# A graph layer with experts: mixing's rows accumulated into x in DRAM, and one expert group of tiles run densely instead of two

## The chip, the cores and the metric

The kernel runs on one core of one Trainium2 chip. The metric is device time in microseconds (us) of one execution; shorter is better. Before the change it is 2823.4 us, the median of three runs (2821.6 to 2824.84).

## The reference

3125 nodes with 512 features, 53125 directed edges (25000 random pairs in both directions, and one loop at each node). Cut to what matters:

```
xn  = layernorm(x)
x   = x + gnn(xn, edges) + mix(xn)
out = x + experts(layernorm(x))

gnn:      two layers; in each, attention over the edges with 8 heads of 64 (softmax over a
          node's incoming edges), Wo, batch norm over the nodes, ff 512->128->512, batch norm;
          after both a layer norm
mix:      linear attention over all nodes; q and k are softmaxed, out = (q ctx)/den + q, then Wp
experts:  p = softmax(z Wg + bg); each node keeps its two best of 8 experts
          out = sum over these e of p_e * (gelu(z W1_e + b1_e) W2_e + b2_e)
```

## The kernel before, in words

Nodes are sorted by their number of edges and cut into 25 tiles of 128 (the last has 53). `FGROUPS` are seven groups of `GT` = 4 tiles, g0 to g6; g6 is the one tile of 53 rows. Two groups, g5 and g6 (`STAY`), remain in SBUF between the steps of a layer, the others go through a DRAM tile `xmid`.

**Edges of the second layer (attention, L508).** A tile's edges are taken in chunks of `G` = 2 slots. For each chunk POOL starts one or two indirect gathers of K and V rows (L591, `lane<-kvd,idx`), DVE multiplies K by q (L596) and sums (L597); after the softmax, ACT (L632) or DVE (L635) weighs V, and TensorE adds up (L647, L652). There are four lanes with six places each; the gather of a chunk goes over the K half of an earlier one, so it waits for its L597, and over the V of one earlier still. POOL takes its instructions in order, as all engines do, so a gather also waits for whatever stands ahead of it there. Beside the edges, in small steps of a generator, runs the mixing: `mixed` (L809 to L858), nine steps for each of 25 tiles. How many steps go between two chunks is a count written in the loop (L891 to L921). Its last step copies the rows y from PSUM on ACT (L856) and stores them to a DRAM tile `base` through SP's queue (L857). Another DRAM tile, `xb`, holds x plus the bias of the mixing and that of the last layer norm, by node; it is written at the start of the kernel (L369).

**After the edges**, batch norms and the ff run over the groups (L926 to L968; L943 is ACT's half of the norm, with scale and bias by feature), in the order g5, g6, g0, ... (`FORDER`). Then `last` (L990):

- `gates(group)` is a generator (L1025). For each tile it turns features to rows (`ps`, TensorE L1044, ACT copy L1046) and takes statistics (`row_stats`, DVE L476, L477). It gathers rows of `base` and of `xb` (two indirect gathers on POOL, L1056) and adds them on POOL (L1059), and forms y on DVE (L1061, L1063), with statistics again. Then z, the normalized rows, on DVE (L1072); z goes to DRAM (`zld`) if the tile is listed; four transposes of z (`tr`, L462) with a copy that alternates between ACT (L454) and DVE (L456); the gate product `pg` (L1080) and its bias (L1082). Then softmax, ranks and the choice of two for the group (L1089 to L1106), and the second biases, comb times b2, added to `yall` (L1108 to L1119). All copies of `pg`, of `pc` and of some others share one PSUM bank.
- Two groups run **densely**, g5 and g4 (`ALL_EXPERTS`): all their nodes go through all eight experts (`all_experts`, L1127: `ph` L1134, gelu L1137, `py` L1141, weighted sum on DVE L1143) and are stored by an indirect DMA (`put`, L1123).
- The other 17 tiles (`LISTED`, `NL`) are **listed**: DVE forms lists of nodes by expert (`lists`, L1149), with a loop of 2 x 17 rounds of one DVE operation (L1217) and one product on `pw` (L1219), which gives `which` (L1222). 40 parts (`PARTS`) of 128 rows then go through one expert each (`one_expert`, L1233): POOL gather of z rows (L1236), transposes and copy (L462, L464), `ph` (L1243), the first bias as a product of a row of ones and b1 in fp32 (L1245), gelu (L1250), transpose `pt` (L1252) and copy (L1253), `py` (L1255), copy (L1257), store to `yld` by SP (L1258).
- In the end, for each listed tile, two gathers from `yld` (L1291), two weighted sums on DVE (L1294) and a put.

The driver (L1260 to L1297) sets the order: gates of g5; gates of the other groups, and after each third `yield` one dense expert of g5; lists; gates of g4 and three of its dense experts; the 40 parts; the five experts that are left, with g4's puts; the final loop over listed tiles. The order within one engine's queue is mostly that of the program, with a scheduler that moves some instructions ahead where their inputs are ready.

Of the kernel before, what the change touches and what calls it, by code (L numbers as in the profile page):

```python
# [1 line left out]

# [55 lines left out]

ALL_EXPERTS = [FGROUPS[STAY[0]], FGROUPS[4]]
LISTED = [t for g in FGROUPS if g not in ALL_EXPERTS for t in TILES[g[0]:g[0] + g[1]]]  # L60
# [32 lines left out]
def gps_layer(ctx: ExitStack, tc: tile.TileContext, x, src, dst, cols, rows,  # L93
# [15 lines left out]
    recd = tc.dram_tile([FT * P, 4], I32, name="recd")  # L109
    base = tc.dram_tile([N, D], F32, name="base")  # L110
    zd = tc.dram_tile([N, D], F32, name="zd")
# [285 lines left out]
    with tc.If(flag < 1) as fits:  # L397
        listed_layers(tc, cols=cols, rec=rec, idx=idx, mask=mask, kvd=kvd, zd=zd, ztd=ztd, xb=xb,
                      base=base, wqo=wqo, layer_weights=layer_weights, **args)
    with fits.Else():  # L400
# [17 lines left out]
def listed_layers(ctx: ExitStack, tc: tile.TileContext, rows,  # L418
                  gnn_wq, gnn_wk, gnn_wv, gnn_wo, gnn_w1, gnn_w2,
                  mix_wq, mix_wk, mix_wv, mix_wp, wg, bg, w1, w2, b2, out,  # L420
                  ident, epst, colt, cols, rec, idx, mask, kvd, zd, ztd, xb, base,
                  wqo, layer_weights):
# [85 lines left out]
    def attention(l, stats, wq, wo, mixw):  # L508
        with tc.tile_pool(name="att", bufs=1, reuse_waits="tile") as ap, \
# [299 lines left out]
            def mixed(t):  # L809
# [46 lines left out]
                nc.scalar.copy(y[:n], ps[:n])  # L856
                nc.sync.dma_start(base[t * P:t * P + n, :], y[:n])  # L857
                yield  # L858
# [113 lines left out]
    def load_experts(fp):  # L972
        w1t = fp.tile([128, NX, NP, FX], F32, name="w1t")
        w2t = fp.tile([FX, NX, D], F32, name="w2t")
        for e in range(NX):
            nc.sync.dma_start(w1t[:, e], w1[e].rearrange("(c p) f -> p c f", p=128))
            nc.sync.dma_start(w2t[:, e, :], w2[e])
        b2t = fp.tile([NX, D], F32, name="b2t")
        nc.sync.dma_start(b2t, b2)
        wgt = fp.tile([128, NP, NX], F32, name="wgt")  # L980
        nc.sync.dma_start(wgt, wg.rearrange("(c p) e -> p c e", p=128))
        bgt = fp.tile([P, NX], F32, name="bgt")
        nc.sync.dma_start(bgt, rows_by_partition(bg, 0, P))
        gt = fp.tile([P, D], F32, name="gt")
        nc.sync.dma_start(gt, rows_by_partition(rows, ROW_G, P))
        b1t = fp.tile([1, NX, FX], F32, name="b1t")
        return w1t, w2t, b2t, wgt, bgt, gt, b1t


    def last(xT, w1t, w2t, b2t, wgt, bgt, gt, b1t):  # L990
        with tc.tile_pool(name="fin", bufs=1, reuse_waits="tile") as fp, \
# [19 lines left out]
                           allow_small_or_imprecise_dtypes=True)  # L1011

            b1p = pp.tile([NX, FX], F32, name="b1p", tag="pg", bufs=1)
            nc.tensor.transpose(b1p, colt[:, XB1:XB1 + NX], ident)
            b1s = fp.tile([NX, FX], F32, name="b1s")
            nc.scalar.copy(b1s, b1p)
            b1d = tc.dram_tile([NX, FX], F32, name="b1d")
            nc.sync.dma_start(b1d, b1s)
            nc.sync.dma_start(b1t, b1d.rearrange("(o e) f -> o e f", o=1))
            steps = fp.tile([P, NL], F32, name="steps")  # L1020
# [4 lines left out]
            def gates(t0, k):  # L1025
# [15 lines left out]
                for i, (t, n) in enumerate(tiles):  # L1041
# [5 lines left out]
                    row_stats(fp, yall[:n, t, :], mv[:n, i, :])  # L1047
                yield
                inv = fp.tile([P, GT], F32, name="sd_y", bufs=2)
                nc.scalar.activation(inv, mv[:, :, 1], AF.Sqrt, bias=epst)  # L1050
                nc.vector.reciprocal(inv, inv)
                for i, (t, n) in enumerate(tiles):
                    bt = fp.tile([P, D], F32, name="bt", bufs=4)
                    bx = fp.tile([P, D], F32, name="bx", bufs=3)
                    for o, held_in in ((bt, base), (bx, xb)):
                        nc.gpsimd.indirect_dma_start(  # L1056
                            out=o[:n], out_offset=None, in_=held_in[:, :],
                            in_offset=bass.IndirectOffsetOnAxis(ap=node(t), axis=0))
                    nc.gpsimd.tensor_add(bt[:n], bt[:n], bx[:n])  # L1059
                    y = yall[:n, t, :]  # L1060
# [4 lines left out]
                    row_stats(fp, y, mv2[:n, i, :])  # L1065
                yield
                sd = fp.tile([P, GT], F32, name="sd_z", bufs=2)
                nc.scalar.activation(sd, mv2[:, :, 1], AF.Sqrt, bias=epst)
                nc.vector.reciprocal(sd, sd)
                for i, (t, n) in enumerate(tiles):  # L1070
                    z = fp.tile([P, D], F32, name="z", bufs=3)
                    nc.vector.tensor_scalar(z[:n], yall[:n, t, :], mv2[:n, i, 0:1], sd[:n, i:i + 1],  # L1072
                                            op0=OP.subtract, op1=OP.mult)
# [8 lines left out]
                    nc.vector.tensor_add(prob[:n, i, :], pg[:n], bgt[:n])  # L1082
                yield

                prob, rank = prob[:, :k, :], rank[:, :k, :]
                m = fp.tile([P, GT], F32, name="pm", bufs=2)
                m = m[:, :k]
                wide = [P, k, NX]
                nc.vector.tensor_reduce(m, prob, AX.X, OP.max)  # L1089
# [7 lines left out]
                for e in range(NX):  # L1097
                    more = fp.tile([P, GT, NX], F32, name="more", bufs=2)
                    pe = prob[:, :, e:e + 1]
                    nc.vector.tensor_tensor(more[:, :k, :e + 1], pe.to_broadcast([P, k, e + 1]),  # L1100
                                            prob[:, :, :e + 1], OP.is_gt)
                    if e + 1 < NX:
                        nc.vector.tensor_tensor(more[:, :k, e + 1:], pe.to_broadcast([P, k, NX - 1 - e]),
                                                prob[:, :, e + 1:], OP.is_ge)
                    nc.vector.tensor_add(rank, rank, more[:, :k, :])
                nc.vector.scalar_tensor_tensor(prob, rank, 1.5, prob, op0=OP.is_lt, op1=OP.mult)  # L1106
                yield
                combT = fp.tile([NX, GT * P], F32, name="combT")  # L1108
# [4 lines left out]
                nc.vector.tensor_copy(combT[:, :w], pc[:, :w])  # L1113

                for i, (t, n) in enumerate(tiles):
# [3 lines left out]
                    nc.vector.tensor_add(yall[:n, t, :], yall[:n, t, :], pb[:n])  # L1119
                yield prob  # L1120

# [27 lines left out]
            def lists():  # L1149
# [8 lines left out]
                    for a, b in ((0, 2), (2, 3), (3, 5), (5, 7))]  # L1158
                both = both[0]

                end = LISTED[-1][1]
# [47 lines left out]
                room = xT.tiles[2].rearrange("p c r -> p (c r)")  # L1209
                hot = room[:, 4 * P:4 * P + 2 * NL * PARTS].rearrange("p (j q) -> p j q", q=PARTS)  # L1210
                nc.vector.tensor_tensor(hot, digf[:, 1, :, None].to_broadcast([P, 2 * NL, PARTS]),
# [3 lines left out]
                for j in range(2 * NL):  # L1215
                    low = room[:, j % 4 * P:(j % 4 + 1) * P]
# [16 lines left out]
            def one_expert(part, e, which):  # L1233
# [25 lines left out]

            def weights(g):  # L1260
                for prob in gates(*g):
                    pass
                return prob

            work = all_experts(*ALL_EXPERTS[0], weights(ALL_EXPERTS[0]))
            ready = 0
            for g in FGROUPS:
                if g not in ALL_EXPERTS:
                    for _ in gates(*g):
                        ready += 1  # L1270
                        if ready % 3 == 0:
                            next(work, None)
            for _ in work:
                pass
# [11 lines left out]
            for _ in work:  # L1286
                pass
            for u, (t, n) in enumerate(LISTED):
                for i in range(2):
                    y1 = xT.tiles[3][:, (2 * u + i) % 4, :]  # L1290
                    nc.gpsimd.indirect_dma_start(  # L1291
# [624 lines left out]
```

## Time and profile before

| | |
|---|---|
| median of three runs | 2823.4 us |
| profiled execution, its own time | 2825.41 us |
| its span | 2823.7 us |
| TensorE busy | 2319.8 us, 82% |
| VectorE (DVE) busy | 2029.8 us, 72% |
| ScalarE (ACT) busy | 1394.9 us, 49% |
| GpSimd (POOL) busy | 1482.8 us, 53% |
| TensorE clock, mean | 0.888 of full |

The profile is one execution, slightly longer than the median. Its span runs from the first to the last recorded instruction. Stages, in us from the span's start: edges of the second layer 1336 to 2240, norms and ff to 2327, gates to 2516, ranks and lists to 2544, the loop on `pw` to 2570, up to the first part to 2607, the parts to 2729, the tail to the end. In a row of a timeline stand start, duration, engine, line, operation, output and inputs, and in brackets how long the engine had been idle and what ended that. PE is TensorE's product, PEld its weight load. fp32 products are recorded as two instructions each. A row of waits reads: engine, tile and line that waited, what for, total us, times, longest.

### The profile page before, as it was taken

The page shows a single profiled execution, that of the slowest core. Times are in us where ns is not written, and L with a number is a line of the kernel's source. Part 1 is how long each engine was busy: PE and PEld are TensorE (multiplying, and loading weights), DVE is VectorE, ACT ScalarE, POOL GpSimd, SP SyncE. Part 2 cuts the span into 40 slices and gives each one's busy share as a digit, 9 for nine tenths or more (in the row PEclk, how much of TensorE's full clock was granted, in tenths as well). Part 3 has the DMA queues.
Part 4 walks back from the last instruction along what each step waited for, and adds up shares of the span by engine and source line. Part 5 has one row for each costly group of instructions (what it writes and reads, how often), then busy time and mean ns, then how long its engine had stood idle before and what let it go on. Part 6 is the DMA issues. An engine that isn't in the chain of part 4 may idle for free. (4 is left out here: it accounts for less than half of the span.)

```text
span 2823.7 us, 31795 instructions
## 1 busy us (share of the span) xinstructions
PE 2319.8 (82%) x9096; PEld 1306.3 (46%) x9096; DVE 2029.8 (72%) x3245; ACT 1394.9 (49%) x5341; POOL 1482.8 (53%) x1231
## 2 busy tenths in 40 slices
PE   6987989889889867999697788888977576869992
PEld 3432435545445544344345455555544334436750
DVE  7810989999999986401879888999987577774333
ACT  1111578788777753201467677787766333211210
POOL 3261788888777860011657666666765205420336
PEclk9998999999999988999799898989989787766996
DMA  8434989999999874422978888989977513210554
GB/s 286 169 119 142 336 324 332 330 329 334 341 327 341 319 238 149 163 80 80 321 257 310 294 319 285 333 302 327 329 269 252 158 32 103 88 56 29 170 152 148
DMA packets 229275, 654.54 MB, mean 232 GB/s; under 512 B 50968, under 2 KB 56477, under 8 KB 224991
## 3 DMA queue, kind: packets, MB, share of 16 engines
q0 software_dynamic: 168352, 537.28, 54.6%
q1 hardware_dynamic: 58184, 110.16, 10.7%
q10 hardware_dynamic: 2556, 4.97, 0.5%
q8 instruction: 77, 1.26, 0.2%
q14 instruction: 106, 0.87, 0.1%
HBM read 562.90 MB, written 89.54 MB: 231 GB/s over the span
## 5 line engine op out<-in xcount | busy, mean ns | idle before, releaser
L591 POOL DMA_INDIRECT lane<-kvd,idx x906 | 1141.1, 1259 | 528.3 <-issue 187.5
L632 ACT ACTIVATE lane<-lane,sc 128x64 f32<-128x64 f32 x3888 | 945.3, 339 | 117.0 <-DVE sc L622 113.9
L596 DVE TENSOR_TENSOR lane<-lane,q 128x1024 f32<-128x1024 f32 (+1 forms) x464 | 548.4, 1191 | 156.7 <-DMA lane<-kvd,idx 142.1
L652 PE MATMUL agg<-ident,lane 128*128 128x128 f32 (+1 forms) x3272 | 527.1, 298 | 144.2 <-DVE lane L635 59.6
L652 PEld LDWEIGHTS agg<-ident,lane 128*128 128x128 f32 (+1 forms) x3272 | 417.4, 153 | 322.5 <-ACT lane L632 149.2
L597 DVE TENSOR_REDUCE sc<-lane 128x16 f32<-128x1024 f32 (+1 forms) x464 | 545.0, 1186 | 2.4 <-ACT lane L632 1.4
L635 DVE TENSOR_TENSOR lane<-lane,sc 128x1024 f32<-128x1024 f32 (+1 forms) x214 | 252.1, 1196 | 0.1
L563 PE MATMUL pq<-wq,xg 128*128 128x512 f32 (+1 forms) x400 | 205.6, 645 | 18.0 <-ACT kt L742 12.4
L709 PE MATMUL po<-aT,wo 128*128 128x512 f32 (+1 forms) x448 | 196.7, 579 | 21.0 <-ACT aT L696 14.0
L502 POOL DMA_INDIRECT kvd<-kv,rec x25 | 24.7, 988 | 221.1 <-DVE kv L499 215.2
L709 PEld LDWEIGHTS po<-aT,wo 128*128 128x128 f32 x448 | 81.1, 204 | 99.1 <-issue 65.5
L499 DVE COPY kv<-pv 128x512 f32<-128x512 f32 (+1 forms) x25 | 17.3, 692 | 151.8 <-PE pv L496 151.8
L563 PEld LDWEIGHTS pq<-wq,xg 128*128 128x128 f32 (+1 forms) x400 | 75.0, 204 | 94.6 <-issue 70.6
L1236 POOL DMA_INDIRECT xT<-zld,which x40 | 38.1, 954 | 151.2 <-PE tr L462 96.7
L380 ACT COPY kv<-pkv 128x512 f32<-128x512 f32 (+1 forms) x50 | 29.1, 584 | 165.6 <-PE pkv L378 140.7
L378 PE MATMUL pkv<-wk,xT 128*128 128x512 f32 (+1 forms) x200 | 100.8, 638 | 7.5 <-ACT kv L380 7.5
L728 PE MATMUL pq<-wmk,zT 128*128 128x512 f32 (+1 forms) x200 | 99.4, 616 | 6.8 <-ACT kt L742 4.7
L728 PE MATMUL pq<-wmp,mqT 128*128 128x512 f32 (+1 forms) x200 | 96.5, 624 | 5.1 <-ACT mqT L851 4.4
L728 PE MATMUL pq<-wmv,zT 128*128 128x512 f32 (+1 forms) x200 | 96.7, 599 | 1.9 <-DVE vt L781 1.2
L742 ACT ACTIVATE mq<-pq,hm 128x64 f32<-128x64 f32 (+1 forms) x200 | 59.4, 320 | 67.3 <-DVE hm L739 67.2
L378 PE MATMUL pkv<-wv,xT 128*128 128x512 f32 (+1 forms) x200 | 91.7, 599 | 0.0
L728 PE MATMUL pq<-wmq,zT 128*128 128x512 f32 (+1 forms) x200 | 91.5, 595 | 0.0
(339 smaller groups left out, 3364.2 us busy)
## 6 DMA issues: line engine op xcount, KB each, us to landing
lane<-kvd,idx POOLq DMA_INDIRECT x906, 6.3
kvd<-kv SPq DMA_DIRECT2D x24, 512.0 KB, 2.6
zT<-ztd SPq DMA_DIRECT2D x48, 256.0 KB, 5.6
xmid<-xg SPq DMA_DIRECT2D x10, 1024.0 KB, 5.8
xT<-xmid POOLq DMA_DIRECT2D x10, 1024.0 KB, 8.5
yld<-y SPq DMA_DIRECT2D x40, 256.0 KB, 3.6
xr<-in_x SPq DMA_DIRECT2D x24, 256.0 KB, 3.7
xb<-xo SPq DMA_DIRECT2D x24, 256.0 KB, 5.4
```

The lines of the kernel that those rows point to most:

```text
L378: nc.tensor.matmul(ps[:n], lhsT=xT[t][:, c, :n], rhs=wkv[name][:, c, :], start=(c == 0), stop=(c == NP - 1))
L563: nc.tensor.matmul(ps[:n], lhsT=of_place(t, c), rhs=wq[:, c, :], start=(c == 0), stop=False)
L591: gets.append(nc.gpsimd.indirect_dma_start(out=kv[:n, k, :], out_offset=None, in_=kvd[l][:, :], in_offset=bass.IndirectOffsetOnAxis(ap=idx ...
L596: nc.vector.tensor_mul(ks, ks, self.q[:n, None, :].to_broadcast([n, g, D]))
L597: nc.vector.tensor_reduce(self.sc[:n, :, j:j + g].rearrange("p h g -> p g h"), ks.rearrange("p g (h d) -> p g h d", h=H), AX.X, OP.add)
L632: nc.scalar.activation(v[:, k, h, :], v[:, k, h, :], AF.Copy, scale=self.sc[:n, h, j + k:j + k + 1])
L635: nc.vector.tensor_mul(v, v, self.sc[:n, :, j:j + g].rearrange("p h g -> p g h")[:, :, :, None] .to_broadcast([n, g, H, DH]))
L652: nc.tensor.matmul(self.agg[:, c * n:(c + 1) * n], lhsT=kv[:n, k, c * 128:(c + 1) * 128], rhs=ident[:n, :n], is_transpose=True, start=firs ...
L709: nc.tensor.matmul(ps[:, :w], lhsT=wo[:, kk, c * 128:(c + 1) * 128], rhs=aT[gi][:, kk, :w], start=(kk == 0), stop=(kk == NP - 1))
L728: nc.tensor.matmul(ps[:n], lhsT=lhs(c), rhs=w[:, c, :], start=(c == 0), stop=(c == NP - 1 and bias is None))
L742: nc.scalar.activation(oh[:, h, :], ph[:, h, :], AF.Exp, bias=m[:n, h:h + 1], accum_out=s[:n, h:h + 1])
L1236: nc.gpsimd.indirect_dma_start(out=x1, out_offset=None, in_=zld[:, :], in_offset=bass.IndirectOffsetOnAxis(ap=which[:, part:part + 1], axi ...
```

## The change

1. One dense group, g5; g4's tiles are listed as well: `NL` is 21 and `PARTS` 48.
2. The mixing's y is no longer stored to `base`; it is added to the rows of `xb` in DRAM by an accumulating DMA. Such a DMA is issued by POOL, so L857 moves from SP's queue to POOL's, among the gathers of the edges. `base` goes, and gates gather from `xb` alone, without POOL's addition.
3. `gates` is a plain function without the choice. The driver runs gates of g6, g0 to g4; then the split of b1 (`first_biases`); the choice once for all listed tiles; lists; gates, choice and second biases of g5; four of its experts; the parts; the other four; the final loop. No dense work stands between the gates.
4. z is formed on ACT (scale and bias by row; one more small DVE operation makes the bias), and all copies of `tr` are on ACT.
5. b1 is split into three bf16 rows, and the first bias is one bf16 product instead of one in fp32.
6. The second biases of listed tiles move to the final loop, four tiles at a time.
7. The gathers of the final loop have eight buffers instead of four.

Edits 4, 5 and 6 leave what is computed the same, up to rounding. The diff, cut to its core:

```
-ALL_EXPERTS = [FGROUPS[STAY[0]], FGROUPS[4]]
+ALL_EXPERTS = [FGROUPS[STAY[0]]]
...
                 nc.scalar.copy(y[:n], ps[:n])
-                nc.sync.dma_start(base[t * P:t * P + n, :], y[:n])
+                nc.gpsimd.dma_start(xb[t * P:t * P + n, :], y[:n], accum_op=OP.add)
...
-        b1t = fp.tile([1, NX, FX], F32, name="b1t")
+        b1t = fp.tile([3, NX, FX], BF16, name="b1t")
...
-                    bt = fp.tile([P, D], F32, name="bt", bufs=4)
-                    bx = fp.tile([P, D], F32, name="bx", bufs=3)
-                    for o, held_in in ((bt, base), (bx, xb)):
-                        nc.gpsimd.indirect_dma_start(
-                            out=o[:n], out_offset=None, in_=held_in[:, :],
-                            in_offset=bass.IndirectOffsetOnAxis(ap=node(t), axis=0))
-                    nc.gpsimd.tensor_add(bt[:n], bt[:n], bx[:n])
+                    bt = fp.tile([P, D], F32, name="bt", bufs=6)
+                    nc.gpsimd.indirect_dma_start(
+                        out=bt[:n], out_offset=None, in_=xb[:, :],
+                        in_offset=bass.IndirectOffsetOnAxis(ap=node(t), axis=0))
...
+                nc.vector.scalar_tensor_tensor(mv2[:, :, 0], mv2[:, :, 0], -1.0, sd,
+                                               op0=OP.mult, op1=OP.mult)
                 for i, (t, n) in enumerate(tiles):
                     z = fp.tile([P, D], F32, name="z", bufs=3)
-                    nc.vector.tensor_scalar(z[:n], yall[:n, t, :], mv2[:n, i, 0:1], sd[:n, i:i + 1],
-                                            op0=OP.subtract, op1=OP.mult)
+                    nc.scalar.activation(z[:n], yall[:n, t, :], AF.Identity,
+                                         bias=mv2[:n, i, 0:1], scale=sd[:n, i:i + 1])
...
-                    to_features(pp, "tr", xT[:, :, t * P:t * P + n], z, n)
+                    to_features(pp, "tr", xT[:, :, t * P:t * P + n], z, n, nc.scalar.copy)
...
+            def first_biases():
+
+                b1p = pp.tile([NX, FX], F32, name="b1p", tag="pg", bufs=1)
+                nc.tensor.transpose(b1p, colt[:, XB1:XB1 + NX], ident)
+                left = fp.tile([NX, FX], F32, name="left")
+                nc.scalar.copy(left, b1p)
+                b1s = fp.tile([NX, 3, FX], BF16, name="b1s")
+                b1d = tc.dram_tile([NX, 3, FX], BF16, name="b1d")
+                for i in range(3):
+                    nc.gpsimd.tensor_copy(b1s[:, i, :], left)
+                    nc.gpsimd.tensor_sub(left, left, b1s[:, i, :])
...
-                nc.tensor.matmul(ph, lhsT=ones[0:1, :], rhs=b1t[0:1, bass.ds(e, 1), :],
+                nc.tensor.matmul(ph, lhsT=one[:, :P], rhs=b1t[:, bass.ds(e, 1), :],
                                  start=False, stop=True)
...
-            work = all_experts(*ALL_EXPERTS[0], weights(ALL_EXPERTS[0]))
-            ready = 0
-            for g in FGROUPS:
+            for g in FGROUPS[-1:] + FGROUPS[:-1]:
                 if g not in ALL_EXPERTS:
-                    for _ in gates(*g):
-                        ready += 1
-                        if ready % 3 == 0:
-                            next(work, None)
-            for _ in work:
-                pass
+                    gates(*g)
+            first_biases()
+            choose(lprob, lrank)
             placei, weight, which, experti = lists()
-            work = all_experts(*ALL_EXPERTS[1], weights(ALL_EXPERTS[1]))
-            for _ in range(3):
+            work = []
+            for g in ALL_EXPERTS:
+                prob, rank = gates(*g)
+                choose(prob, rank)
+                second_biases(*g, prob)
+                work.append(all_experts(*g, prob))
+            work = chain(*work)
+            for _ in range(4):
                 next(work)
...
             for u, (t, n) in enumerate(LISTED):
+                if u % GT == 0:
+                    k = min(GT, NL - u)
+                    second_biases(t, k, lprob[:, u:u + k, :])
                 for i in range(2):
-                    y1 = xT.tiles[3][:, (2 * u + i) % 4, :]
+                    y1 = xT.tiles[4 if i else 2][:, u % 4, :]
```

`choose` holds what gates did at L1089 to L1106, and `second_biases` what it did at L1108 to L1119, unchanged but for their widths.

More of the change, by code (lines that the diff above doesn't have):

```diff
@@ L1 @@
 from contextlib import ExitStack
+from itertools import chain
 import concourse.bass as bass
@@ L109, in gps_layer @@
     recd = tc.dram_tile([FT * P, 4], I32, name="recd")
-    base = tc.dram_tile([N, D], F32, name="base")
     zd = tc.dram_tile([N, D], F32, name="zd")
@@ L398, in gps_layer @@
         listed_layers(tc, cols=cols, rec=rec, idx=idx, mask=mask, kvd=kvd, zd=zd, ztd=ztd, xb=xb,
-                      base=base, wqo=wqo, layer_weights=layer_weights, **args)
+                      wqo=wqo, layer_weights=layer_weights, **args)
     with fits.Else():
@@ L420, in listed_layers @@
                   mix_wq, mix_wk, mix_wv, mix_wp, wg, bg, w1, w2, b2, out,
-                  ident, epst, colt, cols, rec, idx, mask, kvd, zd, ztd, xb, base,
+                  ident, epst, colt, cols, rec, idx, mask, kvd, zd, ztd, xb,
                   wqo, layer_weights):
@@ L1011, in last @@
                            allow_small_or_imprecise_dtypes=True)
[L1013 to L1019, printed above, removed]
             steps = fp.tile([P, NL], F32, name="steps")
@@ L1047, in gates @@
                     row_stats(fp, yall[:n, t, :], mv[:n, i, :])
-                yield
                 inv = fp.tile([P, GT], F32, name="sd_y", bufs=2)
@@ L1065, in gates @@
                     row_stats(fp, y, mv2[:n, i, :])
-                yield
                 sd = fp.tile([P, GT], F32, name="sd_z", bufs=2)
@@ L1082, in gates, with choose @@
                     nc.vector.tensor_add(prob[:n, i, :], pg[:n], bgt[:n])
[L1083 to L1088, printed above, removed]
+                return prob[:, :k, :], rank[:, :k, :]
+            def choose(prob, rank):
+                wide = list(prob.shape)
+                k = wide[1]
+                m = fp.tile([P, k], F32, name="pm", tag=f"pm{k}")
                 nc.vector.tensor_reduce(m, prob, AX.X, OP.max)
@@ L1097, in gates, with second_biases @@
                 for e in range(NX):
-                    more = fp.tile([P, GT, NX], F32, name="more", bufs=2)
+                    more = fp.tile(wide, F32, name="more", tag=f"more{k}", bufs=2)
                     pe = prob[:, :, e:e + 1]
-                    nc.vector.tensor_tensor(more[:, :k, :e + 1], pe.to_broadcast([P, k, e + 1]),
+                    nc.vector.tensor_tensor(more[:, :, :e + 1], pe.to_broadcast([P, k, e + 1]),
                                             prob[:, :, :e + 1], OP.is_gt)
                     if e + 1 < NX:
-                        nc.vector.tensor_tensor(more[:, :k, e + 1:], pe.to_broadcast([P, k, NX - 1 - e]),
+                        nc.vector.tensor_tensor(more[:, :, e + 1:], pe.to_broadcast([P, k, NX - 1 - e]),
                                                 prob[:, :, e + 1:], OP.is_ge)
-                    nc.vector.tensor_add(rank, rank, more[:, :k, :])
+                    nc.vector.tensor_add(rank, rank, more)
                 nc.vector.scalar_tensor_tensor(prob, rank, 1.5, prob, op0=OP.is_lt, op1=OP.mult)
-                yield
+            def second_biases(t0, k, prob):
+                tiles = TILES[t0:t0 + k]
                 combT = fp.tile([NX, GT * P], F32, name="combT")
@@ L1119, in gates @@
                     nc.vector.tensor_add(yall[:n, t, :], yall[:n, t, :], pb[:n])
-                yield prob
+            def first_biases():
[8 more added lines that the diff above has]
+                    nc.gpsimd.tensor_sub(left, left, b1s[:, i, :])
+                nc.sync.dma_start(b1d, b1s)
+                nc.sync.dma_start(b1t, b1d.rearrange("e i f -> i e f"))
             def put(t, n):
@@ L1159, in lists @@
                 both = both[0]
+                lows = [room[:, 8 * NL * NX + i * P:8 * NL * NX + (i + 1) * P] for i in range(4)]
                 end = LISTED[-1][1]
@@ L1209, in lists @@
                 room = xT.tiles[2].rearrange("p c r -> p (c r)")
-                hot = room[:, 4 * P:4 * P + 2 * NL * PARTS].rearrange("p (j q) -> p j q", q=PARTS)
+                hot = room[:, :2 * NL * PARTS].rearrange("p (j q) -> p j q", q=PARTS)
                 nc.vector.tensor_tensor(hot, digf[:, 1, :, None].to_broadcast([P, 2 * NL, PARTS]),
@@ L1215, in lists @@
                 for j in range(2 * NL):
-                    low = room[:, j % 4 * P:(j % 4 + 1) * P]
+                    low = lows[j % 4]
                     nc.vector.tensor_scalar(low, iota, digf[:, 0, j:j + 1], number[:, j // 2:j // 2 + 1],
@@ L1258, in one_expert @@
                 nc.sync.dma_start(yld[part * P:(part + 1) * P, :], y1)
-            def weights(g):
-                for prob in gates(*g):
-                    pass
-                return prob
-            work = all_experts(*ALL_EXPERTS[0], weights(ALL_EXPERTS[0]))
-            ready = 0
-            for g in FGROUPS:
-                if g not in ALL_EXPERTS:
-                    for _ in gates(*g):
-                        ready += 1
-                        if ready % 3 == 0:
-                            next(work, None)
-            for _ in work:
-                pass
-            placei, weight, which, experti = lists()
-            work = all_experts(*ALL_EXPERTS[1], weights(ALL_EXPERTS[1]))
-            for _ in range(3):
+            for g in FGROUPS[-1:] + FGROUPS[:-1]:
+                if g not in ALL_EXPERTS:
+                    gates(*g)
+            first_biases()
+            choose(lprob, lrank)
+            placei, weight, which, experti = lists()
+            work = []
[6 more added lines that the diff above has]
+            for _ in range(4):
                 next(work)
```

## The prediction

> **What bounds the kernel now.** I read the page first, then stages by windows, then waits, then two timelines. The profiled execution took 2825.41 us with a span of 2823.7; the median of the three runs is 2823.4, so I sum against 2825.4 and take off 2 at the end. A difference of 0.2% (5.6 us) is about what a measurement can tell from none.
>
> The page: POOL's largest group is the gathers of the edges, and "issue" (its in-order queue, no operand) is much of its idle time.
>
> ```profile
> span 2823.7 us, 31795 instructions
> L591 POOL DMA_INDIRECT lane<-kvd,idx x906 | 1141.1, 1259 | 528.3 <-issue 187.5
> ```
>
> Windows of the stages the change touches: second layer's edges; gates of 21 tiles with a dense group between; ranks, lists and the loop on `pw`; from `which` to the first part; 40 parts; tail. (Columns: stretch, length, then busy time of each engine, granted clock, DMA share.)
>
> ```profile
> core 0: us, PE busy (x) PEld busy (x) DVE busy (x) ACT busy (x) POOL busy (x), PEclk, DMA share, GB/s
> 1336.00:2240.00 904.00, 725.13 (x3029) 438.48 (x3027) 762.06 (x1009) 606.75 (x2515) 562.75 (x456) 0.88 0.81 287
> 2327.00:2516.00 189.00, 143.69 (x512) 81.03 (x513) 138.94 (x412) 50.82 (x77) 82.56 (x72) 0.74 0.30 89
> 2516.00:2570.00 54.00, 36.53 (x125) 25.15 (x124) 38.79 (x145) 7.38 (x12) 3.93 (x4) 0.57 0.05 20
> 2570.00:2607.00 37.00, 36.89 (x103) 20.91 (x104) 16.02 (x50) 6.18 (x9) 6.72 (x7) 0.71 0.17 50
> 2607.00:2729.00 122.00, 121.56 (x664) 86.29 (x663) 37.76 (x82) 30.72 (x76) 31.43 (x33) 1.00 0.51 156
> 2729.00:2824.00 95.00, 34.69 (x76) 13.34 (x74) 39.06 (x55) 3.44 (x5) 59.29 (x55) 0.75 0.48 151
> ```
>
> In the edges DVE is busy 762 of 904 us. Of its 142 idle, most is waiting for gathers (total, times, longest), and gathers themselves wait:
>
> ```profile
> POOL lane L591 <- issue: 107.6, 259, 7.5
> DVE lane L596 <- DMA lane<-kvd,idx: 97.6, 49, 11.8
> POOL lane L591 <- PE agg L652: 67.1, 64, 8.1
> POOL lane L591 <- DVE sc L597: 32.6, 37, 4.1
> ```
>
> **1. Mixing's stores go from SP to POOL (L857): +22 us (0 to +60).** Removed: 25 SP issues and `base`, hidden before. Added: 25 accumulating stores in POOL's queue, each behind its `y` (ACT L856), with gathers behind it that DVE waits for. The trace has no accumulating store. The nearest POOL row is the plain load L1317 at 0.535 us; with 0.30 of issue gap, 0.83 each, 21 in all. The wait I got by laying the changed order over the old times: with 17, 30, 44, 56 ... 423, 439 of 453 gathers ahead of the stores, I took the end of the last of these against the end of the `y` copy. 14 stores come early and wait 7.4, 7.0, 2.6, 0.4, 4.8, 1.8, 2.3, 2.4, 3.4, 2.9, 3.1, 2.4, 0.4 and 3.1 us, two more wait 5.2 and 3.1 where POOL idled anyway, and nine wait 0. That is 52 us, with the issues 73; less the 14 in which POOL idled anyway, 59 us of push on the gathers. A chunk lands a median 2.6 us before DVE L596 takes it; taking each one's slack off leaves 32 us by which DVE gets data late. 97.6 of DVE's 142 idle us are such waits (69%), and other waits swallow the rest: 0.69 x 32 = 22. Ends: 0, if slack and other waits take all; 60, if none. The read of the old rows is 6.4 MB: at the window's 287 GB/s, 22 us of DMA time. I cost it at nothing, as the DMA share is 0.81; with that cover gone it is the price.
>
> The Trainium skill, "DMA: Bandwidth & Descriptors", section "Issuing engines are not separate DMA queues", says that choosing another issuing engine saves only sequencer time, usually small beside the transfer. By it this term would be about 0 and my sum 22 lower; the "issue" row above, 107.6 us in which gathers wait for POOL's queue, speaks against it.
>
> **2. Gates, no dense group between: -44 (-70 to -15).** Before, 189 us hold gates of 21 tiles and g5's eight dense experts. Gates of one group, in the old trace:
>
> ```profile
> 2343.64 3.23 DVE L1072 TENSOR_SCALAR z<-yall,mv,sd_z 128x512 f32<-128x512 f32 x3
> 2345.96 1.94 PE L462 MATMUL tr<-ident,z 128*128 128x128 f32 x8 [16.27 <-DVE z L1072]
> 2347.72 1.88 PE L1080 MATMUL pg<-wgt,xg 128*128 128x8 f32 x8
> 2350.33 1.72 PE L1080 MATMUL pg<-wgt,xg 128*128 128x8 f32 x8
> 2352.79 1.71 PE L1080 MATMUL pg<-wgt,xg 128*128 128x8 f32 x8
> ```
>
> One gate product takes 1.7 us here and four transposes 1.05, at clock 0.5 (2327 to 2360). The order of the change gives a loop with no slack: transposes of y, statistics, two DVE passes and statistics again (9.2 us after the last tile's first statistics, which come 7.05 into a period), root and reciprocal 0.8, z, then transposes and gate products, which stand ahead of the next group's. z on ACT: the nearest row, L943's 128x512, 0.80 against L1072's 0.545; in the chain for the first z only, +0.3. Period 27.2 us at clock 0.5, 21.9 at 1.0. With 9 for the 53 rows and 25.5 for the first full group: 9 + 25.5 + 4 x 27.2 = 143, and 2 for the way in: 145. POOL loses 21 additions of 1.27 and 21 gathers, already off this chain: nothing.
>
> The Trainium skill, "TensorE: Matmul & The Clock Gate", section "What's actually happening", says the clock doubles after one short window, about 3.4 us, of sustained work. By it the dense stretches run fast, and the term is up to 21 lower. In the rows above TensorE works almost gapless from 2346 to 2358, and the clock of that stretch still was 0.5.
>
> **3. Ranks once, lists, loop: +11 (0 to +16).** Before 28 + 26: the 28 hold the ranks of the last group, the lists and the second dense group's passes on DVE. After, one chain of ranks 21 tiles wide, the lists, and g5's passes, the same number of operations: 29. The loop: four rounds with a w1 product between start 3.41 us apart (2551.77, 2555.18, 2558.59), and go from 34 rounds to 42: 10.4 x 3.41 = 36. Sum 65 against 54.
>
> **4. To the first part: +7 (0 to +12).** Before 37. Five parts' transposes and the second biases stand ahead as before; g5 comes as the only dense group, with one more expert ahead (4 products, 0.85 us each on DVE) and a landing.
>
> **5. Parts: +9 (+4 to +23).** 40 took 122 us: 3.05 each, PE busy 121.6 of it. The bias as one bf16 product instead of fp32's two records (0.48 for the pair) saves about 0.32, from the row L565 (384 ns for 512 columns, so some 0.1 for 128): 48 x 2.74 = 131. The upper end is no saving: 145.
>
> **6. Tail: +23 (+10 to +30).** Before: POOL runs 55 issues 1.495 apart while dense experts go on under it.
>
> ```profile
> 2731.37 3.70 PE L1141 MATMUL py<-w2t,hT 128*128 128x512 f32 x8
> 2732.68 0.95 POOL L1291 DMA_INDIRECT xT<-yld,placei  x1 [20.58 <-DMA yld<-y]
> 2734.91 3.60 PE L1134 MATMUL ph<-xT,w1t 128*128 128x512 f32 x8
> 2813.31 1.58 POOL L1123 DMA_INDIRECT out<-yall,rec  x1 [6.11 <-DVE yall L1294]
> ```
>
> After, eight gathers go ahead (eight buffers now), but next in POOL's queue are the four stores of g5, and these need the last of the four experts left: 4 x (3.6 + 3.7) = 29, a little of it past already: POOL gets to them 28 us into the tail. DVE can't add a listed tile meanwhile, as the 16 sums of these experts (L1143) stand ahead of the first addition in its queue. Then 4 stores 5.5, 55 more issues at 1.38 (their spacing where nothing waits) 76, and 8.8 to the end as before: 118 against 95.
>
> **Sum:** 22 - 44 + 11 + 7 + 9 + 23 = +28; 2825.4 + 28 = 2853, less 2 = 2851.
>
> **Rivals.** *Edges take the stores up* (chance 0.20): waits at L591 for PE 67.1 and DVE 32.6 say that lanes, not POOL, often hold a gather; 25 stores then fall into waits. Against it: 97.6 us at L596, and most of the first stores' waits over 2 us. Only +6 of the end stays: 2829, give or take 20.
>
> *TensorE at full clock to the first part* (0.22) is the case on the other side, faster: gates 5 x 5.3 = -26, loop 36 to 18 = -18, way to the first part -10; 54 in all, hence 2851 - 54 = 2797. It decides once more than 28 of these 54 are won. For it: clock 1.00 in the parts, and transposes lie closer in the changed order; against it: 0.50 and 0.57 where gates and lists stood alone.
>
> *Accumulating stores are slow to land and delay gathers behind them* (0.08): 2 us more for each than L857's 5.2, 25 x 2 = 50, less a tenth in slack: 2851 + 45 = 2896. Nothing in the old trace speaks for or against it; that DMA share is 0.81 leaves little room.
>
> **How the numbers follow.** The forecast, 2851 with its own range of 2838 to 2880, has 0.50. The range goes down to the full-clock case and up towards slow stores: 2795 to 2890, leaving out half of the one (0.11), the other (0.06) and a little of the forecast's ends. Faster: 0.22 and 0.06 of the absorbed case, 0.28. Same: 0.05 of that case and 0.02 of the forecast, 0.07. Slower: 0.48 + 0.09 + 0.08 = 0.65.
>
> **What would show it.** Right: in the changed profile POOL waits before L857 for ACT L856, 50 us in sum; L596's wait for gathers grows by 20 or more and the edges by 22; gates 27 us apart at clock 0.5; parts 2.74 apart; 20 or more us of POOL idle before the first store of the tail. Wrong: edges as long as before (first rival); gates 22 apart at 1.0 (second); L857 landing much later than 5.2 us (third); parts still 3.05 apart (the bias saves nothing); a tail under 105 us (the stores did not hold it).

## The result, and the profile after

The changed kernel takes 2840.78 us (median of 20 runs, 2820.97 to 2848.83), the kernel before in the same sittings 2821.99 (20 runs, 2813.54 to 2833.99): a ratio of 1.0066, 95% interval 1.0054 to 1.0078. It is 18.8 us slower. The forecast was 2851, 28 slower. The profiled execution took 2848.34 us, more than the median by 7.6, so the stages below are those of a long one.

From the page of the changed kernel:

```profile
span 2846.6 us, 31732 instructions
...
L591 POOL DMA_INDIRECT lane<-kvd,idx x906 | 1129.1, 1246 | 485.9 <-issue 205.1
```

The windows of the same stages, in the same columns as before: edges of the second layer; gates; ranks and lists; loop on `pw`; way to the first part; parts; tail.

```profile
core 0: us, PE busy (x) PEld busy (x) DVE busy (x) ACT busy (x) POOL busy (x), PEclk, DMA share, GB/s
1335.00:2249.00 914.00, 721.66 (x2980) 435.28 (x2978) 752.93 (x986) 601.88 (x2496) 580.71 (x480) 0.88 0.83 283
2347.00:2482.00 135.00, 73.12 (x338) 66.77 (x339) 64.87 (x186) 43.28 (x76) 22.54 (x22) 0.51 0.27 85
2482.00:2510.00 28.00, 7.87 (x33) 5.90 (x31) 26.65 (x98) 10.65 (x18) 2.08 (x6) 0.56 0.00 1
2510.00:2546.00 36.00, 35.38 (x105) 25.05 (x106) 14.60 (x44) 3.83 (x4) 0.00 (x0) 0.50 0.00 0
2546.00:2595.00 49.00, 46.50 (x133) 25.28 (x133) 20.26 (x56) 6.17 (x11) 8.60 (x9) 0.72 0.17 48
2595.00:2726.00 131.00, 130.24 (x730) 91.35 (x729) 44.41 (x95) 35.90 (x89) 37.11 (x39) 1.00 0.57 173
2726.00:2847.00 121.00, 64.27 (x122) 23.82 (x120) 59.06 (x86) 2.75 (x4) 72.01 (x67) 0.63 0.46 145
```

The gates have given 54 us; the edges, the loop, the way to the first part, the parts and the tail took more than that back. Measured from marks that both traces have (first gather of the layer, last product L596, last norm L943, last gate product of a listed tile, first operation of the loop, `which`, first and last copy of a part), us:

| stage | before | after | difference | forecast |
|---|---|---|---|---|
| up to the edges | 1338.0 | 1335.1 | -2.9 | 0 |
| edges of the second layer | 889.8 | 913.8 | +24.0 | +22 |
| norms and ff | 99.2 | 97.9 | -1.3 | 0 |
| gates | 189.1 | 135.2 | -53.9 | -44 |
| ranks, lists | 28.3 | 28.3 | 0 | +1 |
| loop | 26.0 | 35.9 | +9.9 | +10 |
| to the first part | 39.4 | 49.2 | +9.8 | +7 |
| parts | 119.8 | 130.8 | +11.0 | +9 |
| tail | 94.1 | 120.6 | +26.5 | +23 |
| sum | 2823.7 | 2846.6 | +22.9 | +28 |

In the edges, the waits of the changed kernel: more for POOL's queue, more of DVE for gathers, and the new waits of the stores. These are waits for y, also where the row names another line of ACT: at 17 of the 25 stores POOL stands idle first, and the store starts 0.30 us after the end of y's copy.

```profile
POOL lane L591 <- issue: 123.3, 270, 8.3
DVE lane L596 <- DMA lane<-kvd,idx: 115.4, 58, 11.6
...
POOL xb L857 <- ACT my L856: 25.1, 6, 8.4
POOL xb L857 <- ACT lane L632: 20.7, 10, 3.6
```

The rows of the store itself (durations least, median and most, in ns; then landing in us):

```profile
L857 POOL DMA_DIRECT2D xb<-my x25: 965/987/1020, 1367.4 to 2193.9; - x25
...
DMA to landing us min/median/max: 3.9/5.4/7.1
```

An accumulating issue keeps POOL for 0.99 us, not the 0.53 of the plain load; it lands about as fast as the plain store on SP's queue did (a median of 5.4 us against 5.2).

In the gates, TensorE's rows of one period: a block of work, then 11 us of waiting for z, which waits for DVE.

```profile
2405.32 2.89 PE L1036 MATMUL ps<-ident,xT 128*128 128x128 f32 x12
2419.58 1.97 PE L462 MATMUL tr<-ident,z 128*128 128x128 f32 x8 [11.38 <-ACT z L1061]
2421.46 1.87 PE L1069 MATMUL pg<-wgt,xT 128*128 128x8 f32 x8
```

And in the tail, the eighth gather on POOL, then 12 us until the dense sums of g5 let its first store go:

```profile
2738.21 0.95 POOL L1297 DMA_INDIRECT xT<-yld,placei  x1 [0.31 <-issue]
2751.30 1.01 POOL L1128 DMA_INDIRECT out<-yall,rec  x1 [12.13 <-DVE yall L1148]
```

### The profile page after: what moved, and what is told of

It reads as the page before. It is cut to its first block, busy times and chain, and to the rows that moved or that the text cites. A ratio compares the mean times of both kernels' runs of the same rounds, so it can differ in the third digit from the quotient of the medians.

```text
span 2846.6 us, 31732 instructions
## 1 busy us (share of the span) xinstructions
PE 2307.3 (81%) x9072; PEld 1319.6 (46%) x9072; DVE 1990.4 (70%) x3065; ACT 1399.8 (49%) x5364; POOL 1457.5 (51%) x1228
## 4 chain that ended last, share of the span: by engine, by line
PE 32%; DVE 20%; DMA 16%; issue 11%; ACT 8%; POOL 4%; DVEq 0%; POOLq 0%; ACTq 0%
DMA lane<-kvd,idx 14%; DVE lane L596 7%; ACT lane L632 6%; DVE sc L597 5%; PE pq L728 4%; PE po L709 3%; PE agg L652 3%; PE pk L496 3%; PE pv L496 3%; POOL lane L591 3%; DVE lane L635 2%; PE tr L462 2%; PE py L1261 2%; PE ph L959 2%; PE ph L1249 2%
## 5 line engine op out<-in xcount | busy, mean ns | idle before, releaser
L591 POOL DMA_INDIRECT lane<-kvd,idx x906 | 1129.1, 1246 | 485.9 <-issue 205.1
L596 DVE TENSOR_TENSOR lane<-lane,q 128x1024 f32<-128x1024 f32 (+1 forms) x464 | 549.1, 1192 | 175.1 <-DMA lane<-kvd,idx 158.0
L1242 POOL DMA_INDIRECT xT<-zld,which x48 | 45.7, 952 | 178.6 <-PE tr L462 110.4
```

The costliest lines, as they stand in the source:

```text
L591: gets.append(nc.gpsimd.indirect_dma_start(out=kv[:n, k, :], out_offset=None, in_=kvd[l][:, :], in_offset=bass.IndirectOffsetOnAxis(ap=idx ...
L596: nc.vector.tensor_mul(ks, ks, self.q[:n, None, :].to_broadcast([n, g, D]))
```

## The experiments

Each ratio is against the kernel before on the same chip, with its 95% interval. The runs were on three chips: e1 to e4, e5 to e8, and e9 to e12. On the first all kernels took some 50 us longer (the kernel before had a median of 2872 there), most of it ahead of the edges; so I compare ratios, and stages from the edges on. A stage is read from one trace of each run; the edges of the same code differ by up to 11 us between traces. Apart from e2 and e12, all start from the changed kernel.

**e1: the store back on SP.**

```
-                nc.gpsimd.dma_start(xb[t * P:t * P + n, :], y[:n], accum_op=OP.add)
+                nc.sync.dma_start(base[t * P:t * P + n, :], y[:n])
...
+                    for o, held_in in ((bt, base), (bx, xb)):
...
+                    nc.gpsimd.tensor_add(bt[:n], bt[:n], bx[:n])
```

> The changed kernel with part 2 undone alone: mixing's rows go to base through SP again, the gates gather both and POOL adds. My theory (stores in POOL's queue hold up the gathers of the edges): the edges, from the first gather to the last product with q, come back from 912.6 to about 889 us, waits of that product for gathers from 115 to about 98; the whole 24 us under the changed kernel, so 2817 or 0.998 of the kernel before; the two gathers and the addition per tile cost the gates at most 5. Rival (the edges are longer because the order on the other engines moved, or because of the accumulated bytes elsewhere): edges stay at 912, 2841 or 1.0066.

Measured: 1.0021 (0.9995 to 1.0047). Edges 896.8 us, the waits of L596 for gathers 89.3. But gates 144.6 instead of 135.2: the second gather and the addition, with four buffers for `bt` again in place of six, cost 9.4 there, twice what I had allowed. So part 2 loses on the edges and gains in the gates.

**e2: the accumulating store alone, in the kernel before.**

```
-                nc.sync.dma_start(base[t * P:t * P + n, :], y[:n])
+                nc.gpsimd.dma_start(xb[t * P:t * P + n, :], y[:n], accum_op=OP.add)
...
-                    nc.gpsimd.tensor_add(bt[:n], bt[:n], bx[:n])
```

> The kernel before with part 2 alone: the accumulating store on POOL, one gather in the gates. My theory: edges 24 us longer, 912, and nothing gained in the gates, since POOL's additions were covered there: 2822 + 24 = 2846, 1.0085. Rival (it is not the store): edges 889, 2822, 1.000. If removing the second gather and the addition helps the gates, up to 10 us come off: 2836.

Measured: 1.0061 (1.0034 to 1.0087). Edges 917.3, 27.5 more than in the profile of the kernel before, and 20.5 more than in e1, which has the store on SP on the same chip; gates 183.5, 5.6 less. The store by itself makes the edges longer.

**e3: a plain store, still on POOL.**

```
-                nc.gpsimd.dma_start(xb[t * P:t * P + n, :], y[:n], accum_op=OP.add)
+                nc.gpsimd.dma_start(base[t * P:t * P + n, :], y[:n])
```

and the two gathers of e1.

> The changed kernel with the store still on POOL, but plain, to base, and two gathers and the addition in the gates. It has the queue and the wait for y, and no accumulation. My theory (place in the queue and the wait): POOL still waits some 45 us for y; the issue is about 0.53 us instead of 0.99, 25 x 0.46 = 11 us less on POOL, a third of which reaches the end: 2837, 1.005. Rival (the reading and adding of the old rows is what costs): as with stores on SP, 2817, 0.998.

Measured: 1.0075 (1.0043 to 1.0108). POOL stands 63.3 us ahead of the stores (52.6 in the changed kernel); an issue takes 0.59 us. Edges 906.2, gates 145.5. Without any accumulation the edges are still 9.4 longer than in e1 on the same chip: the place in POOL's queue costs by itself. The other 11.1 up to e2's 917.3 stand against 10 us of longer issues (25 x 0.40), so this run doesn't show that reading and adding the old rows costs nothing. The late stores of e4 and e10 bound it: they accumulate the same rows, and their edges are 7.7 and 2.7 longer than with the store on SP on the same chip (e1, e9).

**e4: the store six steps later.**

```
-                nc.gpsimd.dma_start(xb[t * P:t * P + n, :], y[:n], accum_op=OP.add)
+                ready.append((t, n, y))
...
+                stored()
                 oT = ap.tile([128, NP, P], F32, name="mqT")
```

where `stored` issues the accumulating stores in `ready`; y has two buffers.

> The changed kernel with each accumulating store issued six steps of the mixing later, behind some eight more gathers from the fifth store on, and two buffers for y. The number of stores and bytes is the same; only the wait goes. My theory: of 45 us in which POOL stands before these stores, the 21 of the first four stay, the rest goes; edges about 12 us shorter than in the changed kernel, 900, and 2829, 1.0025. Rival (issue time and transfers cost, not the wait): 912 and 2841, 1.0066.

Measured: 1.0020 (0.9991 to 1.0049), edges 904.5. The wait is gone at 20 of 25 stores; the first four and one late one still stand 34 us with their wait and issue gaps, and L596 waits less than in the kernel before. Its waits (L813 is the store, L864 the copy of y):

```profile
DVE lane L596 <- DMA lane<-kvd,idx: 93.3, 43, 12.1
...
POOL xb L813 <- ACT my L864: 22.3, 4, 8.8
```

**e5: the last dense experts in the final loop.**

```
-            for _ in work:
-                pass
             for u, (t, n) in enumerate(LISTED):
...
                 put(t, n)
+                if u % 3 == 2:
+                    next(work, None)
+            for _ in work:
+                pass
```

> The changed kernel with the last four dense experts called one after each third listed tile in the final loop, g5's four stores at their end. My theory (in the tail POOL stands idle because those stores are ahead of the listed tiles in its queue and wait for the last dense sums): POOL's 12 us of idle time go, tail 120.6 to about 107, all else as in the changed kernel: 13 us shorter, 1.002 of the kernel before. Rival (the tail is bound by the sums on VectorE or by landings, and POOL would wait elsewhere): tail stays within 4 us of 120.6, 1.0066.

Measured: 1.0004 (0.9988 to 1.0021). Tail 108.2, 12.4 less; POOL goes on without a gap (L1295 gathers, L1128 puts):

```profile
2724.89 1.33 POOL L1295 DMA_INDIRECT xT<-yld,placei  x1 [0.30 <-issue]
2726.53 1.02 POOL L1128 DMA_INDIRECT out<-yall,rec  x1 [0.30 <-issue]
```

**e6: two dense groups again.**

```
-ALL_EXPERTS = [FGROUPS[STAY[0]]]
+ALL_EXPERTS = [FGROUPS[STAY[0]], FGROUPS[4]]
```

> The changed kernel with two dense groups again, g5 and g4 (part 1 undone alone): 17 listed tiles, 40 parts. Theory that one dense group is what pays in this order: parts 131 to 110.5, loop 36 to 26, gates one period shorter, -25, but the way to the first part +15, and in the tail 8 experts more at 7.3 us ahead of the stores, +50 and fewer gathers -11: together -20 -10 -25 +15 +39, about the same, 1.0066 give or take 0.003. Rival (the dense work hides elsewhere, so listing g4 costs what its parts cost): 25 us shorter than the changed kernel, 0.998.

Measured: 1.0047 (1.0027 to 1.0068). Gates 109.7 (-25.5), lists 27.0, loop 25.6, to the first part 69.8 (+20.6), parts 107.7 (-23.1), tail 160.6 (+40.0): as the first theory had it, +0.4 us over these stages. In the changed order a second dense group is neither gain nor loss; listing g4 is paid in parts, loop and gates with what it saves in the tail.

**e7: the first half of the gates given ahead.**

```
                     row_stats(fp, y, mv2[:n, i, :])
+                yield
...
-                    gates(*g)
+                    now = gates(*g)
+                    next(now)
+                    if early:
+                        next(early)
+                    early = now
```

> The changed kernel with the first half of each group's gates (rows, statistics, y) given ahead of the second half (z, transposes, gate product) of the group before. Theory (the period of 25.4 us is one chain through VectorE and then TensorE, with nothing overlapped): TensorE's 14 us of work at half clock set the period, 16 to 18, five times 8 less: gates 135 to 95 to 105, 0.993 of the kernel before. Rival (the order that comes out still has each group's transposes behind the next one's statistics): gates 125 to 135, 1.003 to 1.0066.

Measured: 0.9967 (0.9945 to 0.9989), gates 112.5. That is between the two: of TensorE's 68.5 us of waiting for z, 32.0 are left, so about half the groups overlap in the order that came out.

**e8 and e11: wide products in TensorE's idle time.**

```
+                if listed:
+                    idle = pp.tile([P, 512], F32, name="idle", tag="tr")
+                    for i in range(6):
+                        nc.tensor.matmul(idle, lhsT=ident, rhs=w2t[:, i, :], start=True, stop=True)
                 inv = fp.tile([P, GT], F32, name="sd_y", bufs=2)
```

> The changed kernel with six extra products of 512 columns per group in the 11 us in which TensorE waits for z; their results are not used. It tests what the clock follows in the gates. Theory (the clock goes by the columns that are streamed, and short gate products and transposes do not count enough): the granted clock in the gates rises from 0.51 towards 1.0, gate products go from 1.7 to 0.9 us, the period from 25.4 to about 21, gates -20 and perhaps lists and loop faster too: 1.000 of the kernel before. Rival (the clock stays at a half after any idle time): 0.5, the products fill the idle time, gates +0 to +8, 1.0066 to 1.009.

e8 measured: 1.0067 (1.0049 to 1.0084), gates 135.2, unchanged. In the period looked at, the six products (12 records) took 5.6 us, nearly all at full clock; in the 6 us of idle time after them the clock went back to 0.50, 5.1 us after the last one and before z came.

In e11 there are 13, with `w2t[:, i % NX, :]`.

> The changed kernel with 13 extra products of 512 columns per group in place of six, 12 us, about all of TensorE's wait for z. Theory (clock goes by columns streamed over some microseconds, and gate products and transposes count as idle): the clock is 1.0 when the transposes of z begin and falls to 0.5 some 5 us later, within the same group: the first tile's products at twice the speed, period 25.4 to 22.5 or 23.5, gates -10 to -14, 1.002. Rival (only real idle time lowers it): 1.0 through all of the gates, period 20 to 21, gates -22 to -27, 0.998. If neither: gates unchanged or longer, 1.0066.

e11 measured: 1.0008 (0.9984 to 1.0032), gates 120.1, 15.1 less, 1.1 more than the first theory's upper end. One period of it, cut where the kind of work changes: wide products; transposes and gate products of the first tiles; those of the others and the next group's transposes; wide products, in two windows.

```profile
core 0: us, PE busy (x) PEld busy (x) DVE busy (x) ACT busy (x) POOL busy (x), PEclk, DMA share, GB/s
2399.00:2404.30 5.30, 5.30 (x13) 2.23 (x12) 3.20 (x10) 1.88 (x4) 2.15 (x3) 1.00 0.66 186
2404.30:2408.00 3.70, 3.46 (x30) 3.08 (x29) 0.17 (x1) 3.02 (x5) 0.00 (x0) 1.00 0.69 252
2408.00:2415.50 7.50, 7.50 (x37) 7.14 (x37) 1.97 (x8) 2.34 (x4) 0.00 (x0) 0.50 0.05 19
2415.50:2418.00 2.50, 2.50 (x4) 1.11 (x4) 2.34 (x7) 0.69 (x2) 0.00 (x0) 0.50 0.00 0
2418.00:2428.00 10.00, 10.00 (x24) 4.35 (x23) 7.70 (x19) 2.02 (x4) 4.19 (x4) 0.99 0.38 110
```

TensorE is busy nearly all the time (28.76 of 29.00 us), and the clock falls to a half some 3.5 us after the last wide product, while transposes and gate products go on with one gap of 0.24 us. The rival, that only idle time lowers it, is out.

**e12: the first bias alone, in the kernel before.**

```
-                nc.tensor.matmul(ph, lhsT=ones[0:1, :], rhs=b1t[0:1, bass.ds(e, 1), :],
+                nc.tensor.matmul(ph, lhsT=one[:, :P], rhs=b1t[:, bass.ds(e, 1), :],
```

with b1 in three bf16 rows.

> The kernel before with part 5 alone: the first bias of a part as one bf16 product with b1 in three rows. My step: a part takes 2.75 us instead of 3.05; 40 parts 120 to 108.5, all else as before: 0.996. Rival (TensorE's time a part is set by what it waits for): 3.05 and 1.000.

Measured: 0.9994 (0.9974 to 1.0015). A part takes 2.78 us, 40 take 109.0 instead of 119.8, as the step had it; but the gates went from 189.1 to 194.4, and the interval does not tell the whole from no change. In the old order the splitting's six small POOL operations stand among the first gathers of the gates; that they cause the 5.3 us is not shown.

**e9 and e10: what the others point to.** e9 is e1, e5 and e7 together, e10 is e4, e5 and e7.

> The changed kernel with three edits at once: mixing's rows to base through SP (as in the first run), the last dense experts called in the final loop, and the gates' first half given ahead. If the three are independent: edges 913 to between 890 and 897, gates 135 to 112.5 with up to 9 back for the second gather and POOL's addition, tail 120.6 to 108: 50 us shorter than the changed kernel, 0.990 of the kernel before. If POOL's additions hold the pipelined gates: gates 125 to 130 and 0.995.

> As the run before, but with the accumulating store kept on POOL and issued six steps later, so one gather and no addition in the gates. Theory (what the store costs is mostly the wait for y): edges 900 to 904, gates 112.5, tail 108, 0.990; it beats storing through SP if POOL's additions hold the gates, and loses by 5 to 10 us if the issue of 25 stores counts more.

Measured: e9 0.9914 (0.9883 to 0.9945); edges 889.6, gates 129.2, tail 107.7. e10 0.9904 (0.9870 to 0.9937); edges 892.3, gates 113.2, tail 108.2. Both beat both kernels; the two can't be told apart. In their profiles e9's gates are 16.0 longer than e10's, with the second gather and POOL's additions in them, and its edges 2.7 shorter.

## Why the prediction was right

**Edges.** The mechanism was the one named: stores in POOL's in-order queue, waiting for y, with gathers behind them. 52 us of waiting was forecast from the old times; the trace after has 25.1 and 20.7 us in its two largest rows, and 52.6 with the third (6.8), all of it for y. L596's wait for gathers was to grow by 20 or more, and grew by 17.8. The size is less sure than 22 against 24 looks: the changed kernel, e5, e6, e7, e8 and e11 have the same code up to there, and their edges took 913.8, 903.5, 907.9, 907.2, 914.4 and 908.9 us, 909.3 in the mean. Chip by chip, with one or two traces each: on the first, 917.3 (e2) against 896.8 with the store on SP (e1) and 904.5 with late stores (e4); on the third, 908.9 (e11) against 890.2 (mean of e9 and e12) and 892.3 (e10). The term is 19 to 21 rather than 24, near the forecast 22. Of it 13 to 17 went with the late stores, and 2 to 8 stayed, which hold what the issues cost and the waits that were left. The issue was undersized (0.99 us against 0.53 taken from L1317), and more of the push was absorbed. The first rival, that it would all be taken up, is ruled out by e2; the third, slow landings, by the landing of 5.4 us.

The rule that the prediction cites for this term from the Trainium skill ("DMA: Bandwidth & Descriptors", section "Issuing engines are not separate DMA queues"), that another issuing engine saves only sequencer time, usually small beside the transfer, fits the kind of cost and not its weight here: the transfer hardly changed (5.4 us to land against 5.2), and what the gathers behind the stores paid is time of POOL's queue, 25 issues of 0.99 us and 52.6 us of waiting for y.

**Gates, the step that was mis-sized.** Forecast 145, measured 135.2. The period was 25.4 us, not 27.2, which is 7 of the 10; my chain of single durations was too long. The step "POOL loses 21 additions of 1.27 and 21 gathers, already off this chain: nothing" is wrong: e1 and e3 put them back, and the gates took 9.4 and 10.3 us more; in the old order (e2) taking them away gave 5.6.

**Clock.** It was 0.51 in the gates, 0.50 in the loop, as taken from the old rows. The second rival, full clock up to the first part, did not come. The page of the Trainium skill that speaks for it, "TensorE: Matmul & The Clock Gate", section "What's actually happening", says that one short busy window of some 3.4 us opens the clock. In nine periods of e8 and e11 the clock opened 0.5 to 2.9 us after the first wide product; but 14 us of narrow products without a gap did not open it. What the rule calls busy is not what the busy column shows.

**Ranks, loop, parts.** 64.2 against 65 and 130.8 against 131. The part's cadence of 2.77 us (2.74 forecast) is shown to be the bias's work by e12.

**To the first part.** +9.8 against +7. The clock stayed at 0.5 for the first 10 us of this stage. In e1, e9, e10 and e11 the stage took 40.9 to 41.5 us, in e3, e4, e5, e7 and e8 48.2 to 51.1; what sets the two apart is the clock in its first 10 us, 0.91 to 0.96 in the short ones and 0.50 in the long ones. What decides that is not settled.

**Tail.** The mechanism is shown by e5. POOL came to the first store 25 us after the last part, not 28; the issues from there up to the last took 81 us, as forecast (1.39 apart); what comes behind them, with a wait of 4 us ahead of the last store, took 14.5 and not 8.8.

**Sum.** +28 forecast, +22.9 in the profiled pair, +18.8 in the medians. Errors of the steps cancel in part: the gates gave 10 more than forecast, the way to the first part, the parts and the tail took 8 more. The edges of the profiled execution were 4.5 longer than the mean of the six traces of the same code, about the distance between the last two. That the sum came within 10 us of the medians is in part luck. Parts 3, 4, 6 and 7 of the change have no run of their own; what they give or cost is read from the stages alone.

## What to carry to other kernels

An instruction that is moved to another engine's queue brings its wait with it: lay the new order over the old times, find what stands behind it and who waits for that, and put it where its input is long there. A loop whose halves lie on two engines is a serial chain until the next round's first half stands ahead of this round's second half in the program. When one queue does two kinds of work, let the kind that waits longest stand last.

## What the hardware showed that was not expected

TensorE's clock did not go by how long TensorE was busy. In e8 and e11, products of 512 columns over 128 rows raised it from 0.5 to 1.0 within 0.5 to 2.9 us. In e8 it stayed up for 2.5 to 5.3 us of idle time behind them, in e11, in four periods, for 3.5 to 7.0 us of transposes and products of 8 columns; then it fell, with TensorE busy. While it is up, eight records of a gate product take 1.03 us instead of 1.72, and eight transposes 1.04 instead of 1.97.

Wide products alone do not raise it either. In the kernel before, the second biases are products of 512 columns over only 8 rows (L1117): 7.2 us of them without a gap stayed at 0.50, and the clock rose 4.7 us into the products of 128 rows behind them (the two windows below, in the columns of those above: first the biases, then those products). In the loop on `pw`, one product of 512 columns over 128 rows in every 3.41 us (1.85 us of it) left the clock at 0.50 too. What exactly it goes by, these runs don't show.

```profile
2402.27 7.19 PE L1117 MATMUL pb<-b2t,combT 8*128 8x512 f32 x8 [0.90 <-DVE combT L1113]
...
2402.30:2409.40 7.10, 7.10 (x9) 2.47 (x9) 4.75 (x10) 0.30 (x1) 6.02 (x5) 0.50 0.39 115
2409.40:2414.10 4.70, 4.70 (x7) 2.12 (x7) 2.65 (x4) 0.00 (x0) 4.20 (x5) 0.50 0.63 183
```

An accumulating store kept POOL for 0.99 us against 0.59 for a plain one of the same rows (e3). It landed in 5.4 us, where the plain one on SP's queue took 5.2.
